# Scores of two items, then values of two items: the emission order of an attention loop

## The chip, the cores and the metric

The kernel runs on one core of a Trainium2 chip. The metric is device time in microseconds for one execution: the median of three runs. The profile is of one further execution, taken by the hardware profiler; its span runs from the first to the last instruction.

## What is computed

The input x is 4 images of 128 channels and 64 x 64 pixels, so 4 batches of N = 4096 tokens with C = 128 channels, all in fp32. Two layers follow each other.

```python
# layer 0, per batch; 64-wide projections, softmax over all 4096 tokens
att = softmax(einsum('bmi,bmj->bij', wk @ xf, wq @ xf), axis=2)
x   = x + wo @ einsum('bij,bmj->bmi', att, wv @ xf)
# layer 1, on tokens t = x transposed
h   = ln(t)
s   = (h Wq) (h Wk)^T * 128**-0.5          # causal
t   = t + softmax(s) (h Wv)
# feed-forward: a normalised projection, then a recurrence over tokens
Wx  = batchnorm(ln(t) @ W.T)
y_t = sigmoid(Wx_t + y_{t-1} @ V.T);  out = t + y
```

Layer 0 has M = 64 features per head and no mask. Layer 1 has 128 features and a causal mask. The feed-forward part needs the statistics of all tokens before its recurrence can begin.

## The kernel before

The program holds a fast path, which is what runs, and a general path that a branch at the end skips. The fast path has two phases. The first, the attention phase, computes both attention layers and the input of the recurrence for all batches. The second (from line 700 on) normalises, runs the recurrence in chunks, adds the residual and stores the result.

The attention phase is cut into blocks of 512 query tokens (`BLK`), eight per batch (`g` from 0 to 7). Batch by batch, the eight blocks of layer 0 come first, then the eight of layer 1. A key tile is 128 tokens. An **item** is a pair of key tiles for one block of queries. Each block of layer 0 has 16 items, and its two tiles are t and t + 16, so that the first uses partitions 0 to 63 and the second 64 to 127. Block g of layer 1 has 2g + 2 items; the last two hold the four tiles on the diagonal, which are narrower (512, 384, 256 and 128 queries).

For each item three functions emit instructions:

- `scores` (line 602) issues two matmuls into a two-bank PSUM tile `s_ps` (two buffers) and an exponential on ScalarE into `p` (line 607 for layer 0, 609 for layer 1; four buffers). In layer 0 the contraction is 64 rows and the two matmuls use the two halves of the array's rows. On the diagonal GpSimd masks `p` (line 613).
- `sums` adds `p` on VectorE into `dsum` (lines 631, 633, 639 and 641), for the softmax denominators.
- `values` (line 655) issues two matmuls that accumulate in `acc`. In layer 0 each has 64 output columns, so the two use the two halves of the array's columns. At a block's last item, ScalarE copies `acc` to `agg` (line 658) and VectorE folds `dsum` to `den` (line 660).

At the first item of a block, `rows0` or `rows1` computes the block's query rows (`r_ps`, lines 463 and 477) and copies them on VectorE (465, 479). `tokens0` transposes the block's input to token order (`xT_ps`, 472 and 473). `cols0` and `vals0` prepare keys (`kc_ps`, 450) and values (`v_ps`, 458) of the next batch.

After a block's values comes its finish chain. `project` computes the denominators (`den_ps`, 486), their reciprocals (488), the output projection (`o_ps`, 491) and the residual sum on VectorE (496). `normed` makes the layer norm with VectorE (505 to 508, 513 to 518) and one power on GpSimd (510). Then `transposed` turns the normalised tokens with TensorE and a copy (526, 527). Layer 1's chain has three steps, in `finish1`: project and normalise; transpose, with a store of `xc` to DRAM (555); and the projection `wx_ps` (561), read by VectorE (562) and ScalarE (563). Small matmul results, from rows to wx, share two one-bank PSUM buffers (`misc`).

The loop over slots decides the order in which the work is emitted. In slot s it emits scores and sums of item s, then the values of item s - 2, then one further job: the finish step that is due, or else one from the list `side`. A chain's steps carry delays in slots, and `push` notes the slot at which the next one falls due:

```python
yield 2, lambda: (project(0, b, g, agg, den), norm())   # layer 0
yield 5, lambda: transposed(bs[b].xh[:, ts(g, TPB)], ...)
...
yield 1, first      # layer 1
yield 3, second
yield 1, third
```

The order of emission is a priority and not yet the order on the engines: the framework's scheduler arranges each engine's instructions when the program is built, and after that each engine runs its own in that order, with waits on semaphores between the engines.

Of the kernel before, what the change touches and what calls it, by code (L numbers as in the profile page):

```python
# [342 lines left out]
def fast_path(  # L343
# [78 lines left out]
    with tc.tile_pool(name="batch", bufs=1) as batch, tc.tile_pool(name="rows", bufs=2) as rowp, tc.tile_pool(  # L422
# [20 lines left out]
        def cols0(b, m):  # L443

            if m == 0:
                bs[b].kc = batch.tile([P, N // 2], F32, tag="kc", name="kc")
                bs[b].v = batch.tile([P, NT, M], F32, tag="v", name="v0")
            ps = misc("kc_ps")
            for h in range(2):
                nc.tensor.matmul(  # L450
                    ps[h * M : h * M + M], lhsT=wq0, rhs=xs[:, b, ts(m + h * NB // 2, BLK)], start=True, stop=True
                )
            nc.vector.tensor_copy(bs[b].kc[:, ts(m, BLK)], ps)

        def vals0(b, m):
            ps = misc("v_ps").rearrange("p (j c) -> p j c", c=M)
            for j in range(2 * TPB):
                nc.tensor.matmul(ps[:, j], lhsT=xs[:, b, ts(m * 2 * TPB + j, P)], rhs=wv0, start=True, stop=True)  # L458
            nc.scalar.copy(bs[b].v[:, ts(m, 2 * TPB)], ps)
# [8 lines left out]
        def tokens0(b, g):  # L468

            ps = misc("xT_ps")  # L470
            for j in range(TPB):
                nc.tensor.transpose(ps[:, ts(j, P)], xs[:, b, ds(g * BLK + j * P, P)], ident)  # L472
            nc.scalar.copy(xs[:, b, ts(g, BLK)], ps)
# [99 lines left out]
        items = []  # L573
# [16 lines left out]
        def scores(it):  # L590

            ps = ps_s.tile([P, 2 * BLK], F32, tag="s", name="s_ps")
            rows = bs[it.b].rows
            off = 0
            it.at = []
            for h, (t, q0, n) in enumerate(it.tiles):
                if it.layer == 0:
                    part = slice(h * M, h * M + M)
                    lhsT, rhs = bs[it.b].kc[part, ts(t % (NT // 2), P)], rows[part]
                else:  # L600
                    lhsT, rhs = bs[it.b].xhT[:, ts(t, P)], rows[:, q0:]
                nc.tensor.matmul(ps[:, off : off + n], lhsT=lhsT, rhs=rhs, start=True, stop=True)  # L602
                it.at.append((t, q0, n, off))
                off += n
            it.p = prob.tile([P, 2 * BLK], F32, tag="p", name="p")
            if it.layer == 0:
                nc.scalar.activation(it.p[:, :off], ps[:, :off], AF.Exp, bias=nshift)  # L607
            else:
                nc.scalar.activation(it.p[:, :off], ps[:, :off], AF.Exp, scale=float(P) ** -0.5)  # L609
                for t, q0, n, o in it.at:  # L610
                    if t >= TPB * it.g:

                        nc.gpsimd.affine_select(  # L613
                            out=it.p[:, o : o + P],
                            in_=it.p[:, o : o + P],
                            compare_op=ALU.is_ge,
                            fill=0.0,
                            base=0,
                            pattern=[[1, P]],
                            channel_multiplier=-1,  # L620
                        )

        def sums(it):

            if it.first:
                bs[it.b].dsum = wk.tile([P, 2, BLK], F32, tag="dsum", name="dsum")
            it.den = den = bs[it.b].dsum
            if all(n == BLK for _, _, n, _ in it.at):
                flat = den.rearrange("p a b -> p (a b)")
                if it.first:  # L630
                    nc.vector.tensor_copy(flat, it.p)  # L631
                else:
                    nc.vector.tensor_tensor(flat, flat, it.p, ALU.add)  # L633
                return
            for h, (t, q0, n, o) in enumerate(it.at):
                if it.first:
                    if q0:
                        nc.gpsimd.memset(den[:, h, :q0], 0.0)
                    nc.vector.tensor_copy(den[:, h, q0:], it.p[:, o : o + n])
                else:  # L640
                    nc.vector.tensor_tensor(den[:, h, q0:], den[:, h, q0:], it.p[:, o : o + n], ALU.add)  # L641

        def values(it):

            bt = bs[it.b]
            if it.first:
                bt.acc = ps_a.tile([P, BLK], F32, tag="a", name="acc")
            for h, (t, q0, n, o) in enumerate(it.at):
                if it.layer == 0:
                    dst, lhsT = bt.acc[h * M : h * M + M], bt.v[:, t]  # L650
                    start, stop = it.first, it.last
                else:
                    dst, lhsT = bt.acc[:, q0:], bt.xh[:, t]
                    start, stop = it.first and h == 0, it.last and h == 1
                nc.tensor.matmul(dst, lhsT=lhsT, rhs=it.p[:, o : o + n], start=start, stop=stop)  # L655
            if it.last:
                bt.agg = wk.tile([P, BLK], F32, tag="agg", name="agg")
                nc.scalar.copy(bt.agg, bt.acc)
                bt.den = wk.tile([P, BLK], F32, tag="den", name="den")
                nc.vector.tensor_tensor(bt.den, it.den[:, 0], it.den[:, 1], ALU.add)  # L660

        waiting = []

        def push(slot, chain):
            step = next(chain, None)
            if step:
                waiting.append((slot + step[0], step[1], chain))
# [2 lines left out]
            cols0(0, m)  # L670
        for m in range(NT // (2 * TPB)):
            vals0(0, m)
        SKEW = 2
        side = []
        for s in range(len(items) + SKEW + 16):
            if s < len(items):
                it = items[s]
                if it.first:
                    (rows1 if it.layer else rows0)(it.b, it.g)
                    if it.layer == 0:  # L680
                        side.insert(0, lambda it=it: tokens0(it.b, it.g))
                    elif it.g == 1 and it.b + 1 < B:
                        side += [lambda m=m, b=it.b + 1: cols0(b, m) for m in range(NB // 2)]
                        side += [lambda m=m, b=it.b + 1: vals0(b, m) for m in range(NT // (2 * TPB))]
                scores(it)
                sums(it)
            if 0 <= s - SKEW < len(items):
                it = items[s - SKEW]
                values(it)
                if it.last:  # L690
                    push(s, (finish1 if it.layer else finish0)(it.b, it.g))
            due = [w for w in waiting if w[0] <= s]
            if due:
                w = min(due, key=lambda w: w[0])
                waiting.remove(w)
                w[1]()
                push(s, w[2])
            elif side:
                side.pop(0)()
        assert not waiting and not side  # L700


# [155 lines left out]
```

## Time and profile before

| What | Value |
|---|---|
| Median of 3 runs | 2451.88 us (2450.68 to 2451.99) |
| The profiled execution | 2451.08 us |
| Its span | 2449.4 us |
| Mean granted TensorE clock | 0.991 |
| TensorE busy | 2390.2 us, 98% |
| VectorE busy | 1375.7 us, 56% |
| ScalarE busy | 997.1 us, 41% |
| GpSimd busy | 103.4 us, 4% |

In the profile, PE is TensorE's matmuls, PEld its weight loads, DVE VectorE, ACT ScalarE, POOL GpSimd. A line of a group shows the source line, the engine, the operation, the output and inputs by name, their shapes, and the count; then the time that the group kept its engine busy, the mean duration of one in ns, and the idle time of the engine just before, with what ended it. An fp32 matmul appears as two instructions, and matmuls overlap, so that a mean duration is longer than the distance from one start to the next. In a timeline each line gives the start, the time covered and the count of like instructions that were merged. A few matmul records are missing, so that a count can be smaller than the program's.

### The profile page before, as it was taken

The page shows a single profiled execution, that of the slowest core. Times are in us where ns is not written, and L with a number is a line of the kernel's source. Part 1 is how long each engine was busy: PE and PEld are TensorE (multiplying, and loading weights), DVE is VectorE, ACT ScalarE, POOL GpSimd, SP SyncE. Part 2 cuts the span into 40 slices and gives each one's busy share as a digit, 9 for nine tenths or more (in the row PEclk, how much of TensorE's full clock was granted, in tenths as well). Part 3 has the DMA queues.
Part 4 walks back from the last instruction along what each step waited for, and adds up shares of the span by engine and source line. Part 5 has one row for each costly group of instructions (what it writes and reads, how often), then busy time and mean ns, then how long its engine had stood idle before and what let it go on. Part 6 is the DMA issues. An engine that isn't in the chain of part 4 may idle for free.

```text
span 2449.4 us, 23361 instructions
## 1 busy us (share of the span) xinstructions
PE 2390.2 (98%) x8832; PEld 996.0 (41%) x8832; DVE 1375.7 (56%) x2543; ACT 997.1 (41%) x1108; POOL 103.4 (4%) x207
## 2 busy tenths in 40 slices
PE   7999999999999999999999999999999999999994
PEld 2332345444233235544323234544423324544484
DVE  3666655444666655444566665444466666544445
ACT  3555533333555543333455552332355554233242
POOL 0000010000000000000000001000000000000000
PEclk9999999999999999999999999999999999999997
DMA  4000000000000000000000000000000000000033
GB/s 146 1 1 1 1 5 9 9 5 5 5 1 1 1 1 14 5 9 5 5 1 1 1 1 5 13 5 5 9 1 1 1 1 5 9 9 5 9 138 138
DMA packets 10503, 35.64 MB, mean 15 GB/s; under 512 B 1936, under 2 KB 2704, under 8 KB 8848
## 3 DMA queue, kind: packets, MB, share of 16 engines
q1 hardware_dynamic: 8640, 33.56, 3.5%
q8 instruction: 71, 1.16, 0.2%
q10 hardware_dynamic: 1744, 0.53, 0.1%
q14 instruction: 48, 0.39, 0.0%
HBM read 17.30 MB, written 16.78 MB: 14 GB/s over the span
## 4 chain that ended last, share of the span: by engine, by line
PE 95%; DVE 3%; issue 1%; POOL 1%; DMA 0%; ACT 0%; ACTq 0%; POOLq 0%; DVEq 0%
PE s_ps L602 40%; PE acc L655 38%; PE o_ps L491 2%; PE den_ps L486 2%; PE y_ps L734 2%; PE y_ps L745 2%; PE r_ps L463 1%; PE v_ps L458 1%; PE r_ps L477 1%; PE wx_ps L561 1%; PE kc_ps L450 1%; DVE xr L796 1%; PE xhT_ps L526 1%; PE xT_ps L472 1%; PE xh2T_ps L526 1%
## 5 line engine op out<-in xcount | busy, mean ns | idle before, releaser
L633 DVE TENSOR_TENSOR dsum<-dsum,p 128x1024 f32<-128x1024 f32 x676 | 826.1, 1222 | 566.9 <-ACT p L609 309.7
L607 ACT ACTIVATE p<-s_ps,nshift 128x1024 f32<-128x1024 f32 x512 | 568.1, 1115 | 479.5 <-PE s_ps L602 469.6
L602 PE MATMUL s_ps<-rows,kc 64*128 64x512 f32 x2048 | 570.2, 638 | 0.7 <-ACT p L607 0.4
L655 PE MATMUL acc<-p,v 128*64 128x512 f32 x2048 | 555.7, 617 | 0.0
L609 ACT ACTIVATE p<-s_ps 128x1024 f32<-128x1024 f32 (+2 forms) x288 | 274.1, 953 | 656.6 <-PE s_ps L602 589.0
L602 PE MATMUL s_ps<-rows,xhT 128*128 128x512 f32 (+3 forms) x1152 | 504.0, 561 | 2.2 <-DVE rows L479 2.2
L655 PE MATMUL acc<-p,xh 128*128 128x512 f32 (+3 forms) x1152 | 504.4, 557 | 0.0
L655 PEld LDWEIGHTS acc<-p,xh 128*128 128x128 f32 x1152 | 216.2, 190 | 244.0 <-issue 232.9
L602 PEld LDWEIGHTS s_ps<-rows,xhT 128*128 128x128 f32 x1152 | 209.0, 190 | 228.1 <-issue 171.8
L602 PEld LDWEIGHTS s_ps<-rows,kc 64*128 64x128 f32 x2048 | 156.6, 185 | 342.0 <-issue 308.2
L655 PEld LDWEIGHTS acc<-p,v 128*64 128x64 f32 x2048 | 102.3, 134 | 388.0 <-issue 387.5
L510 POOL TENSOR_TENSOR ln_rstd<-ln_var,mhalf 128x4 f32<-128x4 f32 x64 | 66.3, 1035 | 1355.8 <-DVE ln_var L508 1350.9
L631 DVE COPY dsum<-p 128x1024 f32<-128x1024 f32 x60 | 41.6, 693 | 140.8 <-ACT p L607 73.9
L641 DVE TENSOR_TENSOR dsum<-dsum,p 128x256 f32<-128x256 f32 (+1 forms) x120 | 56.3, 499 | 63.8 <-POOL p L613 63.8
L496 DVE SCALAR_TENSOR_TENSOR xs<-o_ps,recs,xs 128x128 f32<-128x128 f32 x256 | 72.7, 343 | 20.5 <-PE o_ps L491 20.5
L486 PEld LDWEIGHTS den_ps<-ones,den 128*128 128x128 f32 x512 | 64.3, 191 | 38.5 <-DVE dsum L633 22.7
L518 DVE TENSOR_SCALAR xh<-xs,ln_mv,ln_rstd 128x128 f32<-128x128 f32 x256 | 71.2, 341 | 2.0
L613 POOL TENSOR_SCALAR_AFFINE_SELECT p<-p 128x128 f32<-128x128 f32 x128 | 35.6, 304 | 768.3 <-ACT p L609 768.3
L486 PE MATMUL den_ps<-ones,den 128*128 128x1 f32 x512 | 63.9, 246 | 0.0
L734 PE MATMUL y_ps<-wn,ident 128*128 128x256 f32 x192 | 58.5, 393 | 5.4 <-issue 5.4
L505 DVE BATCH_NORM_STATS2 ln_st<-xs 128x6 f32<-128x128 f32 x256 | 63.4, 269 | 0.0
L513 DVE TENSOR_TENSOR ln_z<-ln_rstd 128x4 f32<-128x4 f32 x64 | 10.4, 163 | 68.4 <-POOL ln_rstd L510 68.4
(92 smaller groups left out, 1099.7 us busy)
## 6 DMA issues: line engine op xcount, KB each, us to landing
xs<-in_x SPq DMA_DIRECT2D x16, 512.0 KB, 8.2
x<-xc SPq DMA_DIRECT2D x32, 256.0 KB, 2.0
xr<-x SPq DMA_DIRECT2D x4, 2048.0 KB, 14.5
out_x<-xr SPq DMA_DIRECT2D x8, 1024.0 KB, 6.0
wk<-in_c_wkT ACTq DMA_DIRECT2D x2, 32.0 KB, 4.8
wo<-in_c_woT ACTq DMA_DIRECT2D x2, 32.0 KB, 4.3
wqT<-in_a_wqT ACTq DMA_DIRECT2D x1, 64.0 KB, 4.3
wkT<-in_a_wkT ACTq DMA_DIRECT2D x1, 64.0 KB, 5.6
```

The costliest lines, as they stand in the source:

```text
L486: nc.tensor.matmul(dp[:, j : j + 1], lhsT=den[:, ts(j, P)], rhs=ones, start=True, stop=True)
L496: nc.vector.scalar_tensor_tensor(t, in0=op[:, ts(j, P)], scalar=rec[:, j : j + 1], in1=t, op0=ALU.mult, op1=ALU.add)
L505: nc.vector.bn_stats(st[:, j], xs[:, b, ds(g * BLK + j * P, P)])
L510: nc.gpsimd.tensor_tensor(y, var, mhalf, ALU.pow)
L518: nc.vector.tensor_scalar(dst[:, j], xs[:, b, ds(g * BLK + j * P, P)], mv[:, j, 0:1], y[:, j : j + 1], ALU.subtract, ALU.mult)
L602: nc.tensor.matmul(ps[:, off : off + n], lhsT=lhsT, rhs=rhs, start=True, stop=True)
L607: nc.scalar.activation(it.p[:, :off], ps[:, :off], AF.Exp, bias=nshift)
L609: nc.scalar.activation(it.p[:, :off], ps[:, :off], AF.Exp, scale=float(P) ** -0.5)
L633: nc.vector.tensor_tensor(flat, flat, it.p, ALU.add)
L641: nc.vector.tensor_tensor(den[:, h, q0:], den[:, h, q0:], it.p[:, o : o + n], ALU.add)
L655: nc.tensor.matmul(dst, lhsT=lhsT, rhs=it.p[:, o : o + n], start=start, stop=stop)
L734: nc.tensor.matmul(ps, lhsT=ident, rhs=wn[:, s, ts(g, GB)], start=True, stop=False, skip_group_check=True)
```

## The change

The loop now takes two items in one step. A step emits scores and sums of items s and s + 1, then the values of items s - 2 and s - 1, then up to two further jobs. A finish step counts as due if its slot is at most s + 1, and a step's successor is pushed with slot s, the even one. All blocks have an even number of items, so a pair never straddles two blocks. Nothing else is changed: the functions, the delays and the buffers are as they were.

```diff
-        SKEW = 2
         side = []
-        for s in range(len(items) + SKEW + 16):
-            if s < len(items):
-                it = items[s]
+
+        for s in range(0, len(items) + 16, 2):
+            for it in items[s : s + 2]:
                 if it.first:
                     (rows1 if it.layer else rows0)(it.b, it.g)
...
                 scores(it)
                 sums(it)
-            if 0 <= s - SKEW < len(items):
-                it = items[s - SKEW]
+            for it in items[s - 2 : s] if s else []:
                 values(it)
                 if it.last:
                     push(s, (finish1 if it.layer else finish0)(it.b, it.g))
-            due = [w for w in waiting if w[0] <= s]
-            if due:
-                w = min(due, key=lambda w: w[0])
-                waiting.remove(w)
-                w[1]()
-                push(s, w[2])
-            elif side:
-                side.pop(0)()
+            for _ in range(2):
+                due = [w for w in waiting if w[0] <= s + 1]
+                if due:
+                    w = min(due, key=lambda w: w[0])
+                    waiting.remove(w)
+                    w[1]()
+                    push(s, w[2])
+                elif side:
+                    side.pop(0)()
```

## The prediction

> **What bounds the kernel now.** I read the busy times first, then the groups, then the timeline of TensorE in each kind of stage, then who waits for whom.
>
> Busy times (name, busy us, share of the span, instructions), and three of the groups (busy us, mean ns of one | idle time before):
>
> ```profile
> PE 2390.2 (98%) x8832; PEld 996.0 (41%) x8832; DVE 1375.7 (56%) x2543; ACT 997.1 (41%) x1108; POOL 103.4 (4%) x207
> ...
> L633 DVE TENSOR_TENSOR dsum<-dsum,p 128x1024 f32<-128x1024 f32 x676 | 826.1, 1222 | 566.9 <-ACT p L609 309.7
> ...
> L602 PE MATMUL s_ps<-rows,kc 64*128 64x512 f32 x2048 | 570.2, 638 | 0.7 <-ACT p L607 0.4
> L655 PE MATMUL acc<-p,v 128*64 128x512 f32 x2048 | 555.7, 617 | 0.0
> ```
>
> TensorE is never idle in the attention part: only something that shortens its own stream can help, and anything that makes it wait costs in full. An fp32 matmul is two instructions, so an item (two score and two value matmuls) is four plus four. The timeline of TensorE in layer 0 (start us, us):
>
> ```profile
> 201.02 1.13 PE L602 MATMUL s_ps<-rows,kc 64*128 64x512 f32 x4
> 202.08 1.08 PE L655 MATMUL acc<-p,v 128*64 128x512 f32 x4
> 203.09 1.13 PE L602 MATMUL s_ps<-rows,kc 64*128 64x512 f32 x4
> ...
> 209.29 0.66 PE L472 MATMUL xT_ps<-ident,xs 128*128 128x128 f32 x4
> 209.88 1.99 PE L602 MATMUL s_ps<-rows,kc 64*128 64x512 f32 x8
> 211.80 1.08 PE L655 MATMUL acc<-p,v 128*64 128x512 f32 x4
> ```
>
> From start to start, a score group of one item takes 202.08 - 201.02 = 1.06 us, a value group 1.01 us. But where two items' scores happen to stand together (x8), they take 211.80 - 209.88 = 1.92 us, not 2.12: the second item adds 0.86. So each score group carries 0.20 us of fixed cost. For values, the same answer for the end of layer 0:
>
> ```profile
> 319.59 1.93 PE L655 MATMUL acc<-p,v 128*64 128x512 f32 x6
> 321.45 1.77 PE L602 MATMUL s_ps<-rows,xhT 128*128 128x512 f32 x4
> ```
>
> Three matmuls, 1.86 us: 1.01 for the pair, and 0.86 for the third, though it has no partner. A value group so carries 0.15 us fixed, and a half-width matmul without a partner costs as much as a pair, 0.86. In layer 1 all shapes are 128x128; there four instructions take 1.72 us wherever they stand.
>
> [...] Scores in layer 0 use 64 rows, values 64 columns, so each item changes mode twice; the trace agrees, with 0.20 and 0.15 us. [...] The tail of the attention part agrees:
>
> ```profile
> 2316.43 1.16 PE L491 MATMUL o_ps<-wv,agg 128*128 128x128 f32 x8
> 2318.04 1.10 PE L526 MATMUL tT_ps<-ident,xs 128*128 128x128 f32 x4 [0.45 <-DVE xs L496]
> ...
> 2322.41 1.24 PE L526 MATMUL xh2T_ps<-ident,xh 128*128 128x128 f32 x4 [3.27 <-DVE xh L518]
> ...
> 2324.52 2.05 PE L561 MATMUL wx_ps<-xhT,wf 128*128 128x512 f32 x2 [0.87 <-DVE xhT L527]
> ```
>
> After 3.27 us of idling, wx takes 2.05 instead of the usual 1.02 us. The same lines show what a finish costs bare: transposes of xh wait for VectorE's normalisation, wx for a copy.
>
> **Part 1, grouping in layer 0.** I counted groups of like mode in the order of the two built programs. Row-tiled groups: 482 before, 267 after. Column-tiled: 531 and 298 (the kc matmuls are among them). Returns to full mode: 152 and 137, at about 0.2 (a rows matmul takes 1.06 after values, 0.86 otherwise). Saved: 215 x 0.20 + 233 x 0.15 + 15 x 0.2 = 43 + 35 + 3 = 81 us.
>
> **Part 2, split pairs.** The built order isn't what the loop says: at each layer-0 block's end the scheduler puts values of item 14 and one half of item 15, then the next block's four scores, then the other half. Groups with an odd number of matmuls: 20 before, 82 after, so 10 and 41 pairs are torn. 31 x 0.86 = 27 us lost. Check on one layer-0 block: before, 14 score groups at 1.06, one double at 1.92, 16 value groups at 1.01 and 4.15 of others (rows 1.06, two transposes at 0.59, den 0.84, o 1.07) make 37.1; the o_ps of successive blocks stand 37.10 apart in the trace. After: 8 x 1.92 + 8 x 1.87 + 1.01 + 4.15 = 35.5. 1.6 x 32 blocks = 52 us, against 81 - 27 = 54 with the other stages.
>
> Does layer 0 stay free of waits? Score buffers are two: item s+2's scores need exp(s). Scores of a pair end at 1.92, exp(s) at 2.27 (it starts at 1.16, 1.11 long), exp(s+1) at 3.42; the next scores start at 1.92 + 1.87 = 3.79 and 4.75. VectorE needs 2 x 1.22 of 3.79 us. At a block's end its queue is sum(14), sum(15), den, rows: ready at 5.95, needed at 6.72. The xh transposes come 8.65 us after o_ps, xh is ready at 7.9 (7.86 before, one sum between). No wait, by 0.3 us or more.
>
> **Part 3, finishes in layer 1.** A double step runs two due jobs, and delays of 1 now fall due at once: project follows its values directly, and wx its transposes. Between o_ps and the xh transposes TensorE used to have 11.7 us of work (from start to start, blocks 3 to 6 of a batch); in the built order it has 0.97 + 0.86 + 1.72 + 3.44 + 0.44 = 7.43. VectorE's chain in the kernel before, around o_ps at 456.70:
>
> ```profile
> 456.70 1.14 PE L491 MATMUL o_ps<-wv,agg 128*128 128x128 f32 x8
> ...
> 457.87 1.13 DVE L496 SCALAR_TENSOR_TENSOR xs<-o_ps,recs,xs 128x128 f32<-128x128 f32 x4 [0.82 <-PE o_ps L491]
> ...
> 460.41 1.01 POOL L510 TENSOR_TENSOR ln_rstd<-ln_var,mhalf 128x4 f32<-128x4 f32 x1 [14.96 <-DVE ln_var L508]
> ...
> 461.53 1.22 DVE L633 TENSOR_TENSOR dsum<-dsum,p 128x1024 f32<-128x1024 f32 x1
> ...
> 463.26 1.12 DVE L518 TENSOR_SCALAR xh<-xs,ln_mv,ln_rstd 128x128 f32<-128x128 f32 x4
> ```
>
> It ends 7.68 us after o_ps with one sum inside. The new order has two inside, one partly under POOL's 1.01 us: I get 7.86 for the last xh. The wait is about 0.15, plus 0.1 for the copy ahead of wx (one score half, 0.86, is put before wx to hide copy and latency): 0.25 us, in blocks g = 4 to 6. Block 3 has values of the next batch (1.73 us) as cover: 0. Block 2: a kc copy and both sums come first, xh at 9.7 against 8.5: 0.9. Block 1: both sums stand ahead of the variance, 1.3. Block 7: about 1.0, in three batches.
>
> Block 0 is the worst. Its finish meets that of layer 0's block 7: two normalisations queue on VectorE. Before, o_ps of the second came 5.0 us after the first (334.57, 339.58), its xh ended 14.7 after the first, and the transposes came 18.8 after. Now TensorE arrives 10.95 us after the first o_ps (0.97 + 0.84 + 2.15 + 0.86 + 0.97 + 2.58 + 0.44 + 2.15), while VectorE's queue is nearly the same: last xh at 14.6. Wait 3.35; then wx bare behind its copy 0.95; then the next transposes wait for wx's two readers to free the small-PSUM buffer, 0.65. Sum 4.95. Behind it stand the scores of the next block, so all of it lengthens the span. The pattern resembles the tail's, so the clock may halve: up to 2.5 us more a batch; I take half.
>
> Sum: 4 x (4.95 + 1.3 + 0.9 + 0.75) + 3 x 1.0 = 34.6 us, clock 5: 39.6 us lost. Against a saving of 81 - 26.7 = 54.3 that nets -14.7. The profiled execution's own time is 2451.08, 1.7 over its span of 2449.4, and 0.8 under the median; 2451.9 - 14.7 gives **2437 us**. Nothing is moved past a DMA that matters: the stores of xc follow their transposes, with the queue otherwise empty. The delays of the layer-0 chain stay about two items and six.
>
> **Rivals.** *The waits hide.* If VectorE clears earlier, only part 1 and 2 count: 2452 - 54 = 2398. Against it: the chain of 6.7 us with no sum at all still leaves block 0 late. Half hidden is 2418. Chance 0.15. *The waits cancel the gain*: five more us a batch, a clock halved for longer: 2447 to 2457, chance 0.13. *Slower*: at one place, the xh transposes of layer 1, one more sum of 1.22 us gets before the normalisation in each of 32 blocks, because exp gives up its p earlier than I traced: 32 x 1.22 = 39, so 2476. It decides from 0.6 us a block (19.6 / 32). For it: VectorE's order is fixed and waits in line. Against it: my trace already has both sums that can come. Chance 0.15. *No grouping* isn't possible, the built order shows fours. My own forecast, 2418 to 2447, gets 0.57.
>
> 0.2% (4.9 us) is about what a measurement of this kernel can tell from no change. Faster 0.72, same 0.13, slower 0.15. The unknown values: the column group of two items, 1.87, is seen only as a group of three matmuls (bounds 1.87 and 2.02, worth 233 x 0.15 = 35 us; I take 1.87, as the next weights' load in that group, with its wait satisfied, cost nothing); the clock 0 to 10 us; the layer-1 waits 15 to 60 us. Range 2412 to 2455.
>
> **What would show it.** Right: score groups of eight at 1.92 us, value groups of eight at 1.87, layer-0 blocks 35.5 apart; TensorE waits for xh (L518) near 13 us, and for xhT (L527) and the wx readers some us in block 0 of each batch. Wrong: value groups near 2.0, blocks at 36 or more, TensorE waiting for exp or rows in layer 0, or waits for xh above 2 us in blocks 3 to 6.

## The result: the gain in layer 0 is there, and the finishes of layer 1 give it back

The changed kernel takes 2456.03 us (median of four runs, 2451.79 to 2456.89) against 2451.28: a ratio of 1.0016, 95% interval 0.9999 to 1.0033. That is no change that can be measured. The forecast was 2437, with a range up to 2455; the time lies 1 us above it.

The totals on the page of the changed kernel answer to those of before (2390.2 for TensorE, 570.2 and 555.7 for layer 0's matmuls):

```profile
PE 2374.5 (97%) x8832; PEld 1049.2 (43%) x8832; DVE 1387.9 (57%) x2543; ACT 968.3 (39%) x1108; POOL 117.5 (5%) x207
...
L655 PE MATMUL acc<-p,v 128*64 128x512 f32 x2048 | 534.2, 610 | 0.0
L602 PE MATMUL s_ps<-rows,kc 64*128 64x512 f32 x2048 | 526.5, 619 | 0.7 <-ACT p L607 0.4
```

Layer 0's matmuls cover 65 us less (570.2 + 555.7 - 526.5 - 534.2), yet TensorE is busy only 15.7 us less and the span is 5.4 us longer (2454.8). So the grouping works, and something else fills the room. The timeline of TensorE over one layer-0 block (start us, us):

```profile
214.61 1.99 PE L602 MATMUL s_ps<-rows,kc 64*128 64x512 f32 x8
216.53 1.94 PE L655 MATMUL acc<-p,v 128*64 128x512 f32 x8
...
234.13 1.12 PE L463 MATMUL r_ps<-xs,wk 128*128 128x512 f32 x2
235.18 1.93 PE L655 MATMUL acc<-p,v 128*64 128x512 f32 x6
237.04 1.99 PE L602 MATMUL s_ps<-rows,kc 64*128 64x512 f32 x8
238.96 1.07 PE L655 MATMUL acc<-p,v 128*64 128x512 f32 x2
239.96 0.66 PE L472 MATMUL xT_ps<-ident,xs 128*128 128x128 f32 x4
```

Scores of two items take 216.53 - 214.61 = 1.92 us from start to start, values of two 1.87 (next start 218.40), both as forecast. At the block's end is the torn pair: three matmuls in 1.86 us, and after the next block's scores the fourth alone, 1.00 us. From the o_ps of one block to that of the next it is now 35.49 us, where it was 37.10.

Then the waits of TensorE (releaser, us in total, times, longest) in the changed kernel:

```profile
PE xh2T_ps L526 <- DVE xh L518: 23.8, 15, 3.3
...
PE wx_ps L561 <- DVE xhT L527: 3.5, 4, 0.9
...
PE s_ps L602 <- DVE rows L479: 1.1, 4, 0.4
```

And in the kernel before:

```profile
PE xh2T_ps L526 <- DVE xh L518: 3.3, 1, 3.3
PE wx_ps L561 <- DVE xhT L527: 2.8, 4, 0.9
PE s_ps L602 <- DVE rows L479: 2.2, 4, 1.0
```

In both, 3.3 us of the first and 0.9 of the second stand at the tail. The other 1.9 and 2.2 us of the kernel before are small waits in its attention part, where the prediction has TensorE never idle. Without the tail the changed kernel waits 20.5 us for xh, 2.6 for the copy, 1.1 for rows, and 0.8 once ahead of wx in a block 0: 25.0 us, which is 20.9 more than before. The prediction had summed 34.6. What I missed stands at the step from layer 1 to the next batch's layer 0, in three batches:

```profile
601.38 1.94 PE L655 MATMUL acc<-p,v 128*64 128x512 f32 x8
603.24 0.66 PE L526 MATMUL tT_ps<-ident,xs 128*128 128x128 f32 x4
603.83 1.12 PE L602 MATMUL s_ps<-rows,kc 64*128 64x512 f32 x2
606.45 0.58 PE L526 MATMUL xh2T_ps<-ident,xh 128*128 128x128 f32 x2 [1.50 <-DVE xh L518]
606.96 1.35 PE L602 MATMUL s_ps<-rows,kc 64*128 64x512 f32 x2
608.25 0.69 PE L526 MATMUL xh2T_ps<-ident,xh 128*128 128x128 f32 x2
608.87 2.07 PE L602 MATMUL s_ps<-rows,kc 64*128 64x512 f32 x2
610.87 2.07 PE L561 MATMUL wx_ps<-xhT,wf 128*128 128x512 f32 x2
612.87 2.07 PE L602 MATMUL s_ps<-rows,kc 64*128 64x512 f32 x2
614.87 3.45 PE L655 MATMUL acc<-p,v 128*64 128x512 f32 x8
618.25 1.99 PE L602 MATMUL s_ps<-rows,kc 64*128 64x512 f32 x8
```

The wait is 1.50 us, near what I had allowed. But the scores around it stand alone, one half of a pair at a time, and from 606.96 on each instruction group takes up to twice its time: wx 2.07 instead of 1.02, the eight value instructions 3.45 instead of 1.94. The table by stretches shows why; after the stretch, its length and TensorE's busy time come PEld, DVE, ACT and POOL, then the granted clock, DMA share and GB/s:

```profile
607.70:618.00 10.30, 10.30 (x17) 2.55 (x16) 3.75 (x4) 2.70 (x3) 0.00 (x0) 0.50 0.01 2
618.00:630.00 12.00, 12.00 (x52) 3.82 (x52) 6.65 (x6) 6.36 (x6) 0.00 (x0) 1.00 0.00 0
```

For 10.3 us TensorE never stops, at half clock. The clock record of the trace gives 10.24 us at half speed at this step in each of the three batches (607.70 to 617.94, 1187.99 to 1198.23 and 1768.26 to 1778.50 us, each at 0.50). From o_ps of block 7 to o_ps of the next batch's block 0 it is 50.37 us, after 41.35 before: 9.0 longer, where a layer-0 block should be 1.6 shorter.

### The profile page after: what moved, and what is told of

It is laid out like the page before. It is cut to its first block, busy times and chain, and to the rows that moved or that the text cites. A ratio compares the mean times of both kernels' runs of the same rounds, so it can differ in the third digit from the quotient of the medians.

```text
span 2454.8 us, 23353 instructions
## 1 busy us (share of the span) xinstructions
PE 2374.5 (97%) x8832; PEld 1049.2 (43%) x8832; DVE 1387.9 (57%) x2543; ACT 968.3 (39%) x1108; POOL 117.5 (5%) x207
## 4 chain that ended last, share of the span: by engine, by line
PE 92%; DVE 4%; issue 1%; POOL 1%; ACT 1%; DMA 0%; ACTq 0%; POOLq 0%
PE s_ps L602 38%; PE acc L655 37%; PE o_ps L491 2%; PE den_ps L486 2%; PE wx_ps L561 2%; PE y_ps L733 2%; PE y_ps L744 2%; PE r_ps L463 1%; PE r_ps L477 1%; PE v_ps L458 1%; PE xh2T_ps L526 1%; DVE dsum L633 1%; DVE xr L795 1%; POOL ln_rstd L510 1%; PE xhT_ps L526 1%
## 5 line engine op out<-in xcount | busy, mean ns | idle before, releaser
L607 ACT ACTIVATE p<-s_ps,nshift 128x1024 f32<-128x1024 f32 x512 | 543.1, 1111 | 528.5 <-PE s_ps L602 527.0
L655 PE MATMUL acc<-p,v 128*64 128x512 f32 x2048 | 534.2, 610 | 0.0
L602 PE MATMUL s_ps<-rows,kc 64*128 64x512 f32 x2048 | 526.5, 619 | 0.7 <-ACT p L607 0.4
L602 PE MATMUL s_ps<-rows,xhT 128*128 128x512 f32 (+3 forms) x1152 | 491.3, 562 | 1.1 <-DVE rows L479 1.1
L655 PE MATMUL acc<-p,xh 128*128 128x512 f32 (+3 forms) x1152 | 482.3, 557 | 0.0
L602 PEld LDWEIGHTS s_ps<-rows,kc 64*128 64x128 f32 x2048 | 179.7, 186 | 275.1 <-issue 127.1
L655 PEld LDWEIGHTS acc<-p,v 128*64 128x64 f32 x2048 | 130.8, 137 | 366.3 <-issue 365.8
L613 POOL TENSOR_SCALAR_AFFINE_SELECT p<-p 128x128 f32<-128x128 f32 x128 | 51.4, 435 | 722.6 <-ACT p L609 722.5
L486 PEld LDWEIGHTS den_ps<-ones,den 128*128 128x128 f32 x512 | 62.1, 191 | 23.9 <-issue 23.9
L563 ACT COPY xs<-wx_ps 128x512 f32<-128x512 f32 x32 | 18.7, 585 | 95.6 <-DVE stats L562 95.6
```

The source lines that it names most:

```text
L486: nc.tensor.matmul(dp[:, j : j + 1], lhsT=den[:, ts(j, P)], rhs=ones, start=True, stop=True)
```

## Experiments

Theory A from here on: grouping gains what parts 1 and 2 of the prediction say; the loss is the timing of layer 1's finishes, inside layer 1 and, above all, at the step to the next batch. Its first test does one layer at a time.

**Pairs in layer 0 alone.** The loop takes k items per step, and after the scores emits values until two items are pending:

```diff
+            k = 2 if s >= len(items) or items[s].layer in (0,) else 1
+            for it in items[s : s + k]:
...
+            while len(pend) > 2 or (s >= len(items) and pend):
+                it = pend.pop(0)
                 values(it)
...
+            for _ in range(k):
+                due = [w for w in waiting if w[0] <= s + k - 1]
```

> Items by pairs in layer 0 alone; layer 1 goes item by item, as in the kernel before. Theory A (pairs gain 1.61 us in each layer-0 block, and the loss sits in two places: the finishes inside layer 1, some 25 us, and the step from layer 1 to the next batch's layer 0, about 10.6 us in three batches): the second place stays, since the last block of layer 1 finishes inside layer 0's pairs: 2451 - 52 + 32 = 2431, up to 2437. Rival B (the loss belongs to layer 1 as a whole and comes with its pairs): 2451 - 52 = 2399.

Measured: 2423.93 us, ratio 0.9884 (0.9868 to 0.9901). That is far from B's 2399 and 7 us better than A's lower figure. The waits for xh inside layer 1 are gone, and the interval at the step between batches is still 50.4 to 51.9 us; in the first batch the granted clock is 0.51 from 600.70 to 610.90 us. So the place found in the timeline belongs to layer 0's pairs too: block 7 finishes inside them.

**Pairs in layer 1 alone.** The same loop with `(1,)`.

> Items by pairs in layer 1 alone; layer 0 goes item by item. Theory A: no gain, the loss of the finishes inside layer 1 alone: 2451 + 25 = 2476, or a few us less. The step from layer 1 to layer 0 is as before, with no halved clock there. Rival B: 2451 + 57 = 2508.

Measured: 2487.33 us, ratio 1.0148 (1.0131 to 1.0164). The sign and place are A's: the step between batches takes 41.35 us, as before. The size is missed by 11 us. I had left out the clock, whose mean over the profiled run is 0.988 where the kernel before has 0.991 (an estimate from these means and the spans: 0.012 x 2483.9 - 0.009 x 2449.4 = 7.8 us), and small losses, which no run measures apart, where a score stands alone between other work (in the changed kernel's layer 1, 0.94 us from start to start where it takes 0.86 among its like). The two parts nearly add up: 2423.9 + 2487.3 - 2451.6 = 2459.6 against 2456.0. So no interplay of the layers needs explaining.

**Later finishes.** The changed kernel with larger delays in `finish1`:

```diff
-            yield 1, first
-            yield 3, second
-            yield 1, third
+            yield 2, first
+            yield 4, second
+            yield 2, third
```

> The changed kernel, with the delays of layer 1's finish steps raised from 1, 3, 1 to 2, 4, 2, so that no step of a chain runs in the double step that made it due. Theory A (the finishes come too early for VectorE): the waits of TensorE for xh and its halved clock go, 2456 - 25 - 32 + 5 = 2404. Rival C (the double step in layer 1 costs by itself, by scores torn apart and loads of weights not taken ahead): waits are few, their sum in the changed kernel is 27 us without the last one, so at best 2456 - 24 = 2432.

Measured: 2387.46 us, ratio 0.9738 (0.9722 to 0.9754): 2.6% faster than before, and 17 us below A's own figure. C falls. The waits of TensorE in this kernel:

```profile
PE xh2T_ps L526 <- DVE xh L518: 3.3, 1, 3.3
...
PE wx_ps L561 <- DVE xhT L527: 0.9, 1, 0.9
PE r_ps L477 <- ACT xs L563: 0.6, 3, 0.2
PE s_ps L602 <- DVE rows L479: 0.5, 1, 0.5
```

But for 1.1 us of small waits only the tail's are left, and the mean granted clock is 0.991, as in the kernel before. The middle blocks of layer 1 take 43.22 and 50.09 us again, exactly as in the kernel before (43.74 and 50.60 in the changed one): where every matmul uses the full array and no mode changes, pairs gain nothing. With so few waits left, the prices of the prediction can be tested nearly alone. The built order has 255 row-tiled and 301 column-tiled groups (482 and 531 before), 149 returns to full mode (158, counted after both kinds) and 64 groups of odd size (20): 227 x 0.20 + 230 x 0.15 + 9 x 0.2 - 22 x 0.86 = 62.8 us. The span is 63.3 us shorter (2386.1 after 2449.4). The closeness is in part luck: the kernel before had 4.1 us of small waits outside the tail and this one has 1.1, so some 60 us are left for grouping, and the prices are about 2.5 us too high.

**The same delays without pairs**, as a control:

> The kernel before, item by item, with the delays 2, 4, 2 in layer 1. Theory A (the gain of the paired kernel with these delays comes from grouping; the delays only take away waits that pairs made): the kernel before has no such waits, so no change but for three torn pairs fewer in the built order (14 groups of odd size, not 20), 2451.6 - 2.6 = 2449. Rival D (the delays are the gain): 2440 or less.

Measured: 2444.15 us against 2450.89, ratio 0.9969 (0.9958 to 0.9981). The delays alone give 6.7 us; 2.6 of them are the torn pairs. The traces account for the rest, against what I expected: the kernel before did have waits that the delays take away, 1.9 us for the copy ahead of wx and 1.2 of the 2.2 for rows, and three column groups (0.5 us) and three returns to full mode (0.6) go as well. So of the 64 us at least 57 come from grouping, once nothing spoils it.

**Only block 7's finish later.** Only the last block of each batch in layer 1 gets more delay:

```diff
+            late = 1 if g == NB - 1 else 0
             yield 1, first
-            yield 3, second
-            yield 1, third
+            yield 3 + late, second
+            yield 1 + late, third
```

> The changed kernel, with the transposes and the projection of block 7's finish in layer 1 one slot later (3 to 4, 1 to 2), and nothing else. Theory A1 (the half clock after this block follows from the wait of 1.5 us for xh together with scores that run without a partner): wait 1.5, clock 5.1 and two torn pairs 1.7 go in three batches, 2456 - 25 = 2431. Rival A2 (the clock falls because a block of layer 0 starts with half-empty work, with or without the wait): the half clock stays, 2456 - 3 x 3.2 = 2446.

Measured: 2431.91 us, ratio 0.9922 (0.9906 to 0.9939): 24.1 us below the changed kernel, near A1's 25; two torn pairs per batch, 5.2 us, are part of it. The interval at the step falls from 50.37 to 41.22 us in each of the three batches. One edit of one block's finish so moves more than all waits for xh in the other blocks.

**What lowers the clock.** That edit takes away both the wait and lone scores. Two runs separate them. The first fills the wait with spare matmuls whose result is overwritten:

```diff
+            for _ in range(2 if fill is not None else 0):
+                nc.tensor.matmul(ps, lhsT=wf, rhs=fill, start=True, stop=True)
             for j in range(TPB):
                 nc.tensor.transpose(ps[:, ts(j, P)], src[:, j], ident)
```

> The changed kernel with two spare matmuls (128x512, 0.86 us each, overwritten by the transposes that follow) ahead of the xh transposes of block 7 in layer 1, in three batches: work added where TensorE idles. In the built order one torn pair per batch goes with it. Theory A1 (idling lowers the clock here): the half clock of 10.2 us after this block goes, 2456 - 3 x (5.1 + 0.9) = 2438. Rival A2 (half-empty score work lowers it): 2456 - 3 x 0.9 = 2453.

Measured: 2445.10 us, ratio 0.9975 (0.9967 to 0.9983), between the two figures. The timeline of the first batch, and further down that of the third:

```profile
603.15 1.88 PE L526 MATMUL xh2T_ps<-xhT,wf 128*128 128x512 f32 x4
605.86 1.09 PE L528 MATMUL xh2T_ps<-ident,xh 128*128 128x128 f32 x4 [0.83 <-DVE xh L518]
606.89 1.12 PE L605 MATMUL s_ps<-rows,kc 64*128 64x512 f32 x2
607.94 1.13 PE L564 MATMUL wx_ps<-xhT,wf 128*128 128x512 f32 x2
...
1760.05 1.58 PE L564 MATMUL wx_ps<-xhT,wf 128*128 128x512 f32 x2
1761.56 3.18 PE L605 MATMUL s_ps<-rows,kc 64*128 64x512 f32 x6
```

In the first batch wx runs at full speed (1.13 us), with more work and a wait of 0.83 us left. In the third, wx and the six score instructions after it take 1.58 and 3.18 us, where the first has 1.13 and 1.98. From the start of wx to the next values that is 4.62 us and not 2.97; an estimate from these two, if all of the difference is half clock, is 3.3 us of it. From o_ps to wx both batches have the same instructions at the same distances, within 0.02 us, and what makes them differ was not shown. The second run leaves the wait and puts full-array work where lone scores stood:

```diff
                 wp = misc("wx_ps")
+                for _ in range(4 if g == NB - 1 and b + 1 < B else 0):
+                    nc.tensor.matmul(wp, lhsT=wf, rhs=bs[b].xhT[:, :BLK], start=True, stop=True)
```

> The changed kernel with four spare full-array matmuls (128x512 fp32, 0.86 us each at full clock) written into wx's tile ahead of wx, for block 7 of layer 1 in three batches; the result is overwritten. In the built order they take the place of two lone half-array scores after the wait for xh, so what follows the wait is full-array work without a gap. Theory H [...]: the wait of 1.5 us stays, the half clock after it lasts 3.4 to 6.8 us and not 10.2. Rival [...]: 10.2 us again. Time: 3.4 us of work more per batch, 1 torn pair and 0 to 3.4 us of half clock less: 2453 to 2466.

Measured: 2450.98 us, ratio 1.000 (0.999 to 1.001), so 5 us below the changed kernel although TensorE has 3.4 us more to do in each of three batches. Its timeline at the same place, in the third batch, and below it that of the changed kernel:

```profile
1759.52 1.12 PE L604 MATMUL s_ps<-rows,kc 64*128 64x512 f32 x2
1762.13 0.58 PE L526 MATMUL xh2T_ps<-ident,xh 128*128 128x128 f32 x2 [1.49 <-DVE xh L518]
1762.56 1.02 PE L562 MATMUL wx_ps<-xhT,wf 128*128 128x512 f32 x2
1763.41 0.38 PE L526 MATMUL xh2T_ps<-ident,xh 128*128 128x128 f32 x2
1763.63 2.74 PE L562 MATMUL wx_ps<-xhT,wf 128*128 128x512 f32 x6
...
1764.60 1.12 PE L602 MATMUL s_ps<-rows,kc 64*128 64x512 f32 x2
1767.22 0.58 PE L526 MATMUL xh2T_ps<-ident,xh 128*128 128x128 f32 x2 [1.49 <-DVE xh L518]
1767.73 1.59 PE L602 MATMUL s_ps<-rows,kc 64*128 64x512 f32 x2
```

The wait is the same in both, and yet wx's matmuls take 1.02 us with the spare work. In none of the three batches does the clock fall at this step: the first two wx instructions take 1.02 us and the next six 2.74 in each, and in the first batch the granted clock is 1.00 from 601 to 612 us. That goes beyond both expectations (3.4 us at the least).

So the wait alone doesn't lower the clock here. A wait of 1.49 to 1.50 us with full-array work after it left the clock up in three batches; one as long with lone half-array scores after it was followed by 10.24 us at 0.50 in three batches of the changed kernel. This rests on these two kernels. Whether the moment at which the wait falls has a part in it was not shown, and the two batches of the filled wait, alike up to wx and different from there, speak for something more than the order of the work.

**Which delay.** Only the middle one raised (1, 4, 1):

> The changed kernel with only the middle delay raised (1, 4, 1). Theory A: the waits for xh (20.5 us without the last) and the half clock (44 us at half speed, at most 22) go, and 3 torn pairs (2.6); the waits of wx (2.6) stay, as wx still follows its transposes at once: 2456 - 20 - 22 - 3 = 2411. If the first or last delay carries the loss instead: 2430 or more.

Measured: 2401.33 us, ratio 0.9796 (0.9780 to 0.9813), 10 us better than expected. The middle delay, between the normalisation and the transposes of its result, carries 55 of the 69 us that all three bring. With it alone TensorE still waits 4.5 us in all for the copy ahead of wx, 2.1 for rows and 1.6 for a key copy, and 12 groups stay odd that the full set makes even, 6 x 0.86 = 5.2 us. The full set has 2.0 us of such waits itself, the tail's 0.9 among them, so 6.2 + 5.2 = 11.4 of the remaining 14 us are accounted for.

**No torn pairs.** On top of the larger delays, the rows of the next block are computed one double step early, ahead of the values:

```diff
+            for it in items[s + 2 : s + 3]:
+                if it.first:
+                    (rows1 if it.layer else rows0)(it.b, it.g)
             for it in items[s - 2 : s] if s else []:
                 values(it)
```

> Pairs with the delays 2, 4, 2, and the rows of a block computed one double step earlier, so that the scheduler has no gap before a block's first scores to fill. In the built order no pair is torn any more (64 groups of odd size before). Theory: each torn pair costs 0.86 for the lone half and 0.15 for one more group: 2387.5 - 32 x 1.01 = 2355. If tearing only covered a wait for rows: 2387 or more.

Measured: 2348.67 us, ratio 0.9581 (0.9565 to 0.9597), 6 us better than expected. This is the fastest kernel of the study, 4.2% under the one before. A block's end in its timeline:

```profile
225.43 1.99 PE L602 MATMUL s_ps<-rows,kc 64*128 64x512 f32 x8
227.35 1.12 PE L463 MATMUL r_ps<-xs,wk 128*128 128x512 f32 x2
228.41 1.94 PE L655 MATMUL acc<-p,v 128*64 128x512 f32 x8
230.27 1.99 PE L602 MATMUL s_ps<-rows,kc 64*128 64x512 f32 x8
232.19 1.94 PE L655 MATMUL acc<-p,v 128*64 128x512 f32 x8
```

Between the rows matmul and the first scores that need its result (230.27) a whole group of values now stands, and no group of odd size is left in the trace (64 before): the scheduler has no gap to fill with half a pair. Blocks stand 34.49 us apart, 1.00 less than with the tear, as priced. The rest of the 38.8 us comes from layer 1, where the middle blocks take 0.2 us less each and the passages between the layers shorten as well.

## Why the prediction was wrong

- **Part 1, grouping,** and **part 2, torn pairs,** were right: a layer-0 block gained 1.61 us where 1.6 was worked out, and in the kernel with later finishes the two terms together give 62.8 us, where the span shrank by 63.3, 3.0 of it waits. For the changed kernel they gave 54.3; it should have been 52.5, since the returns to full mode were counted after column-tiled groups only (with those after row-tiled ones they are 158 and 152, not 152 and 137).
- **Layer 0 free of waits** was right: nothing there waits for exp or rows beyond the 0.7 us of before, and xh is ready at 7.68 us after o_ps, needed at 8.64.
- **Part 3, block 0** was right in kind and near in size. Waits of 2.88 us for xh, 0.83 ahead of wx and 0.43 for rows after it stand against 3.35, 0.95 and 0.65 (that last one I had put down to a small-PSUM buffer); the clock falls to 0.50 for 3.41 us (334.66 to 338.07), which costs about 1.7 at most, against 1.25 put down, half of 2.5 that were an assumption and worked out from no trace. The prediction's own figures for the first wait, 14.6 less 10.95, give 3.65 and not 3.35. In the trace the last xh comes at 14.70 and TensorE is ready at 11.11, but it starts on the first of the four xh and so waits only 2.88. Blocks 1 and 2 waited 0.92 and 0.29 us for xh, where 1.3 and 0.9 were put down. Blocks 4 and 5 lost 0.52 us each, not 0.25: half of that is the wait, the rest lies at the lone scores around it.
- **The step that failed is "Block 7: about 1.0, in three batches".** The interval there grew by 9.0 us where it should have shrunk by 1.6, so the loss is 10.6 per batch. Part 2 had counted 2.6 of it (three torn pairs), the wait took 1.5, and up to 5.1 is the half clock (10.24 us at half speed); for the last 1.4, four more score groups at 0.20 are 0.8. 1.0 was to stand for what is 10.6 - 2.6 = 8.0, so 21 us are missing in three batches, and the forecast missed by 19. The run with block 7 alone later took off 24.1. That 21 and 19 are so close is in part luck: in blocks 0 to 6 the waits beyond those of the kernel before came to 16.4 us where 31.6 were put down, and some 10 us that no term held made up for much of it.
- The term for the clock was put at the wrong place. I took the tail's 3.27 us wait for the pattern and asked only of block 0 whether it resembled it. The single scores of block 7 were priced as torn pairs, but not with the 10.24 us of half clock that came with them and the wait.
- Of the rivals, *the waits cancel the gain*, 2447 to 2457 with a chance of 0.13, is what came: a clock halved for longer. It was thought of for block 0. The range ended at 2455, inside it, and should have taken it in whole.

A sum for the changed kernel against the one with later finishes, 68.7 us by the spans: waits 23.9, half clock at most 22 (4 x 3.41 + 3 x 10.24 = 44.4 us outside the tail), nine torn pairs 7.7, twelve more row groups 2.4. Some 13 us remain; lone scores in layer 1 are likely part of it, but no run measured them apart, and the cause of these 13 us stays open.

## What to carry to other kernels

Where matmuls of different tiling alternate, look for a fixed price per group: a timeline shows it as the difference between a doubled group and two single ones (0.20 and 0.15 us here), and grouping earned it. But read the built order and not the loop: a scheduler that filled a gap with half a pair cost a whole pair's time here (0.86 us), and starting the producer of that gap earlier was the cure. When a loop's step is made coarser, delays counted in steps change their meaning; a delay has to be at least the time that the slowest engine's chain needs in the new steps, and a wait on a saturated TensorE can cost more than its length, as here, where the clock was at half for 10.24 us after a wait of 1.50.

## What the runs showed of the hardware

- In the changed kernel a wait of 1.50 us, with lone half-array matmuls before and after it, was followed by a granted clock of 0.50. With full-array matmuls after a wait of 1.49 to 1.50 us the clock stayed up: wx took 1.02 us in each of three batches.
- The half clock outlasted the wait by far: 10.24 us in each of three batches, with TensorE busy all the time. In block 0 of layer 1 it lasted 3.41 us in each of four batches, in the first of them after waits of 2.88 and 0.83 us. What brings the clock back was not shown.
- Two half-array matmuls side by side took the time of one. A group of one lone score took 1.05 us from start to start and a group of one pair 1.06; for values it was 1.00 and 1.01. Without the fixed cost of the group that is 0.85 us for a lone one and 0.86 for a pair, in row and in column tiling.
